# Message passing on sorted edges: one block of the last layer changes from gathered to multiplied

## The chip, the cores and the metric

The kernel runs on one core of a Trainium2 chip. The metric is the device time of one execution in microseconds; the time of a kernel is the median of its runs. The engines are PE (matrix multiplication; PEld is its weight load), DVE, ACT and POOL (elementwise work; POOL issues the indirect gathers here), and SP, which only issues DMAs here.

## The reference

A graph network on 6250 nodes of 256 features and 100000 edges that are sorted by destination. Four times the features of every edge's source are summed at its destination and added to the node's own, and a small network of three dense steps follows; the last of the four has a middle of 64 features.

```python
def agg(h):
    return jax.ops.segment_sum(h[src], dst, num_segments=N)
for l in range(NL - 1):
    h = x + agg(x)
    h = jax.nn.relu(h @ W1s[l] + b1s[l])
    h = jax.nn.relu(h @ W2s[l] + b2s[l])
    x = h @ W3s[l] + b3s[l]
h = x + agg(x)
h = jax.nn.relu(h @ cW1 + cb1)
h = jax.nn.relu(h @ cW2 + cb2)
return h @ cW3 + cb3
```

Ahead of it stands a layer norm with ReLU, and the input is added to the result.

## The kernel before

The nodes are cut into 49 blocks of 128. The sum over edges of a block of destinations is formed in one of two ways.

*Multiplied.* The counts of edges from every node to the block's 128 nodes are a matrix of small integers. It is built once, in layer 0, from one-hot matrices (`build`, L1053 one-hots on DVE, L1094 matmuls on PE, L1102 and L1104 to 8-bit integers on ACT and DVE), stored in HBM (`mats`), fetched again by SP in each layer (`fetch`), cast to the matmul's type (L1582, L1598, ACT and DVE in turn), and multiplied with all node features, which stay in SBUF as a high and a low part (`XY`). In layers 1 to 3 blocks 20 to 47 are multiplied as seven *panels* of four blocks (`product`, L1700, 196 matmuls each). A *solo* is a single block that is multiplied by itself (`product_by_node`, L1622, 49 matmuls); its result is kept until its quad of blocks is complete. In layer 0 blocks 18 to 43 are multiplied one by one on the same line (`teams`), while the build goes on; blocks 44 to 47 are only built there.

*Gathered.* For the other blocks, 17 indirect DMAs on POOL (`send`, L1407) bring the feature rows of 17 x 128 edges each from the layer's table in HBM, and one *visit* on PE (`add`, L1446, 23 small matmuls that the profile shows as 46) sums them with one-hot matrices. Block 48 is the last visit of every layer. Layer 0 has 23 visits, layers 1 and 2 have 20 each, layer 3 has 19 (blocks 0 to 17 and 48), 82 in all.

The sum of a group of four blocks is turned (L1506), and goes through the second dense step (`second`, L1248 in layer 3, L1256) and the third (`halves` L1268, `third` L1310, L1313); the first dense step needs no matmul of its own, since it is folded into the weights of the layer before. `given_out` adds the input (loaded by SP, L1287 and L1280 on DVE, result L1297) in layer 3.

All engines work in an order that the program fixes when it is built. PE's order comes from a planner with a clock of its own, in estimated microseconds: each matmul adds its cost (`passed`), a solo or panel is walked through matmul by matmul, and ahead of each group `meets` asks whether the next visit is due. `begin` plans the layer's gathers evenly, from now until the estimated end of the layer less `TAIL[l]`; `flow` puts a gather on POOL when its time has come, and makes it wait for the matmul that PE has just been given. From `ends[l] + LATE[l]` on, in steps of the walk, all visits left are due. `made` is the order in which blocks are built in layer 0, `order` the order of panels and solos in a layer, `place_of` tells where a built block lies in HBM. `spare` is the memory of `clT`, free after layer 0, in which solos' results and the last layer's weights are put. The lists `solos`, `made`, `order`, `TAIL` and `LATE` are those that the change touches.

Of the kernel before, what the change touches and what calls it, by code (L numbers as in the profile page):

```python
# [10 lines left out]
U8 = mybir.dt.uint8  # L11
# [6 lines left out]
P = 128  # L18
# [378 lines left out]
def sorted_edges(  # L397
# [39 lines left out]
    N, C = x.shape  # L437
    (E,) = src.shape
    NLAYER = W1s.shape[0]
# [27 lines left out]

    gone = [(0, 4), (4, 4), (8, 4), (12, 4), (16, 4), (44, 4), (48, 1)]
    panels = [(20, 4), (24, 4), (28, 4), (32, 4), (36, 4), (40, 4), (44, 4)]
    solos = [[], [19], [19], [18, 19]]  # L470
    stock = panels + [(b, 1) for b in max(solos, key=len)]
    place_of = {b + i: (p, i) for p, (b, n) in enumerate(stock) for i in range(n)}
    S0 = 2 * min(place_of)
# [2 lines left out]
    teams = [(18, 2), (20, 4), (24, 4), (28, 4), (32, 4), (36, 4), (40, 2), (42, 2)]  # L476
    made = [b + i for b, n in teams for i in range(n)]
    for i in range(panels[-1][1]):
        made.insert(6 * i + 5, panels[-1][0] + i)
    assert sorted(made) == sorted(place_of) and sum(gone[-3]) == panels[0][0] and gone[-2] == panels[-1] and all(n == gone[0][1] for _, n in gone[:-1]) and sorted(  # L480
        b + i for b, n in gone[:-2] + gone[-1:] + panels for i in range(n)) == list(range(NT))
    NQ = len(gone)
# [498 lines left out]
    with tc.manual_schedule():  # L981
        with tc.tile_pool(name="prep", bufs=2) as prep, tc.tile_pool(
            name="ps_t", bufs=2, space=PSUM
# [150 lines left out]
        def later(n, fn):  # L1134
            due.append((now[0] + n, fn))
# [378 lines left out]
        EARLY = 8  # L1514
        PRE = (GSUB + EARLY) // 2
        tails = [7] + [panels[-1][1] + gone[-1][1]] * (NLAYER - 1) + [panels[-1][1]]
        order = [[]] + [[0, 1, 2, 19, 3, 4, 5, 6]] * 2 + [[0, 1, 18, 2, 3, 19, 4, 5, 6]]
        order = [[p if p < len(panels) else place_of[p][0] for p in o] for o in order]
        nodes = [b + i for b, n in teams for i in range(n)]
        parts = [(j, 1) for j in range(NT)]  # L1520
# [11 lines left out]
        spare = clT.rearrange("p a q s -> p (a q s)").bitcast(F32)  # L1532
        sums = ps_g.tile([P, W], F32, name="sums")
        MARGIN = 6.0
        TAIL = [10.0] + [-5.0] * (NLAYER - 1) + [10.0]
        LATE = [-8] + [10] * (NLAYER - 1) + [-8]
        COLS, FULL32, TURN, VISIT, BUILD, BURST = 0.457e-3, 1.68e-3, 0.4, 3.0, 0.2, 0.3
        clock = [0.0]
        FAR, SPAN = 7, 6
# [137 lines left out]
        def product(l, p, ps_a):  # L1677
            b0, n = stock[p]
            if n == 1:
                k = solos[l][::-1].index(b0)  # L1680
                u = alone[l, b0] = late.tile([P, C], F32, name="us", bufs=1) if (
                    k == 1) else spare[:, k // 2 * C:(k // 2 + 1) * C]
                return product_by_node(l, (b0,), ps_a, [u], None)
            last = len(panels) - 1
            w = n * P
# [42 lines left out]
        with tc.tile_pool(name="hots", bufs=1) as hots, tc.tile_pool(  # L1728
            name="ats", bufs=1
        ) as ats, tc.tile_pool(name="rings", bufs=AHEAD + 2) as rings, tc.tile_pool(  # L1730
            name="gath", bufs=24
        ) as gath, tc.tile_pool(
            name="ps_a", bufs=2, space=PSUM
        ) as ps_a, tc.tile_pool(name="ps_b", bufs=3, space=PSUM) as ps_b:
            begun = {0: clock[0]}
            rings.tile([P, 64], U8, name="align", bufs=1)
            layers[0].begin()
            layers[0].send(8)
            beside = build(hots, ats, ps_b)
            while now[0] < PRE:  # L1740
                for _ in range(2):
                    next(beside)
                    built[0] += 1
                tick(layers[0])
                layers[0].advance()
            later(1, lambda: later(2, lambda bad=verdict(): judge(bad)))
            for team in teams:
                product_of_team(*team, ps_a, beside, team == teams[-1])
            assert next(beside, None) is None and built[0] == total
        chunks = ctx.enter_context(tc.tile_pool(name="chunks", bufs=1))  # L1750
        late = ctx.enter_context(tc.tile_pool(name="late", bufs=1))
        rings = ctx.enter_context(tc.tile_pool(name="rings2", bufs=AHEAD + 5))
        rings.tile([P, 128], U8, name="align", bufs=1)
        gath = ctx.enter_context(tc.tile_pool(name="gath2", bufs=27))
        ps_a = ctx.enter_context(tc.tile_pool(name="ps_a2", bufs=4, space=PSUM))
        for l in range(1, NLAYER + 1):
# [67 lines left out]
```

## Time and profile before

| | us |
|---|---|
| median of 3 runs (2122.25 to 2134.76) | 2123.33 |
| profiled execution, its own time | 2128.08 |
| its span, first to last instruction | 2126.3 |
| PE's busy time in the span | 2034.3 |
| POOL's busy time in the span | 1445.9 |
| first gather of layer 1 / 2 / 3 | 714.2 / 1194.9 / 1668.4 |

The page has one line for each group of instructions: line, engine, operation, out<-in with shapes, count, then busy time, mean ns of one, and the engine's idle time just before them with what ended it. In the chain of waits a line is start, length and what: the work, followed back from the last instruction, that each step waited for. A line of the timeline gives start, length, engine, line, operation, and in brackets the idle time before it and what ended that. Matmuls overlap, so the mean of one in the page is longer than the time from one to the next, which the chain shows.

### The profile page before, as it was taken

The numbers are of one execution on the slowest core, as the hardware profiler recorded it, in microseconds if no ns is written. First come the engines' busy times: TensorE is split into PE (matmuls) and PEld (weight loads), VectorE is DVE, ScalarE is ACT, GpSimd is POOL, SyncE is SP. The second block draws the span as 40 slices with busy tenths as digits, with TensorE's granted clock in tenths as the row PEclk, the third lists the DMA queues.
The fourth block names the chain that finished last, engine by engine and source line by source line (L and its number), as shares of the span: only waits on it lengthen the run. The fifth ranks groups of instructions, "written<-read, shape, count | busy, mean of one in ns | idle before, by whom it ended". The sixth has DMA issues, their size and how long they took to land.

```text
span 2126.3 us, 33236 instructions
## 1 busy us (share of the span) xinstructions
PE 2034.3 (96%) x12076; PEld 1495.9 (70%) x12076; DVE 925.0 (44%) x2103; ACT 872.8 (41%) x1793; POOL 1445.9 (68%) x1467
## 2 busy tenths in 40 slices
PE   6889999999999999999999999999999999989998
PEld 4657676667676777777777777777776767766665
DVE  6987767677662422232234322322233323223333
ACT  5766656456555433323233423232233322222222
POOL 3747777677774477777777477777776477777772
PEclk9989999999999999999999999999999999999999
DMA  5534455545455654555566554555555555555563
GB/s 174 159 117 148 145 156 150 157 139 162 140 161 168 205 163 145 160 177 161 154 184 202 171 165 149 176 166 158 169 171 176 173 170 185 161 184 185 154 189 109
DMA packets 184900, 347.54 MB, mean 163 GB/s; under 512 B 32446, under 2 KB 118496, under 8 KB 184726
## 3 DMA queue, kind: packets, MB, share of 16 engines
q0 software_dynamic: 68960, 185.36, 29.9%
q1 hardware_dynamic: 113838, 158.12, 22.8%
q8 instruction: 96, 1.57, 0.3%
q10 hardware_dynamic: 1928, 1.85, 0.3%
q14 instruction: 78, 0.64, 0.1%
HBM read 287.93 MB, written 57.26 MB: 162 GB/s over the span
## 4 chain that ended last, share of the span: by engine, by line
PE 86%; DMA 4%; DVE 3%; issue 1%; ACT 1%; POOL 1%; DVEq 0%; SPq 0%; POOLq 0%; ACTq 0%
PE agg L1700 43%; PE agg L1622 15%; PE sums L1446 11%; PE ps L1256 6%; PE ps L1313 6%; PE bp L1094 4%; DMA rows<-table,idx 4%; PE ps L1506 1%; DVE hi L1053 1%; POOL rows L1407 1%; DVE at L1104 1%; PE ps L1268 1%; PE ps L1248 0%; DVE lo L1053 0%; ACT at L1102 0%
## 5 line engine op out<-in xcount | busy, mean ns | idle before, releaser
L1407 POOL DMA_INDIRECT rows<-table,idx x1394 | 1388.8, 996 | 595.7 <-issue 225.7
L1700 PE MATMUL agg<-a,XY 128*128 128x512 f32 x4116 | 978.6, 395 | 1.9 <-DVE clT L1634 1.9
L1700 PEld LDWEIGHTS agg<-a,XY 128*128 128x128 f32 x4116 | 764.9, 188 | 192.7 <-issue 35.0
L1598 ACT CAST a<-at 128x512 fp32r<-128x512 uint8 (+1 forms) x542 | 328.7, 617 | 653.7 <-PE agg L1700 613.1
L1598 DVE CAST a<-at 128x512 fp32r<-128x512 uint8 x543 | 246.8, 456 | 515.7 <-PE agg L1700 479.1
L1622 PE MATMUL agg<-XY,a 128*128 128x512 f32 x1470 | 405.4, 410 | 1.7 <-ACT a L1582 1.0
L1622 PEld LDWEIGHTS agg<-XY,a 128*128 128x128 f32 x1470 | 260.0, 190 | 51.4 <-issue 6.6
L1446 PE MATMUL sums<-rows,hot 128*32 128x256 f32 x3772 | 248.3, 391 | 33.5 <-DMA rows<-table,idx 33.3
L1446 PEld LDWEIGHTS sums<-rows,hot 128*32 128x32 f32 x3772 | 124.0, 111 | 151.0 <-DMA rows<-table,idx 46.1
L1582 ACT CAST a<-at 128x512 fp32r<-128x512 uint8 (+2 forms) x362 | 197.2, 576 | 6.6 <-PE agg L1622 6.6
L1102 ACT CAST at<-bp 128x392 uint8<-128x392 f32 x252 | 121.5, 490 | 186.9 <-PE bp L1094 181.3
L1104 DVE CAST at<-bp 128x392 uint8<-128x392 f32 x228 | 128.6, 564 | 137.4 <-PE bp L1094 135.0
L1475 DVE TENSOR_TENSOR u<-u,sums 128x256 f32<-128x256 f32 x82 | 34.4, 419 | 301.3 <-PE agg L1700 273.6
L1094 PE MATMUL bp<-hi,lo 128*128 128x196 bf16 x960 | 128.3, 256 | 14.9 <-DVE hi L1053 13.3
L1313 PE MATMUL ps<-w,h 128*128 128x256 f32 x588 | 133.8, 379 | 1.4 <-ACT h L1259 0.9
L1053 DVE TENSOR_TENSOR hi<-cols,pairs 128x784 bf16<-128x784 bf16 x240 | 134.9, 562 | 0.0
L1256 PE MATMUL ps<-h,w 128*128 128x512 f32 (+3 forms) x332 | 133.8, 545 | 0.3 <-ACT h L1713 0.3
L1094 PEld LDWEIGHTS <-lo 128*128 128x128 bf16 x960 | 72.3, 100 | 83.5 <-DVE hi L1053 34.9
L1313 PEld LDWEIGHTS ps<-w,h 128*128 128x128 f32 x588 | 111.3, 190 | 18.5 <-ACT h L1259 1.4
L1321 DVE TENSOR_TENSOR zz<-ps,w 128x512 f32<-128x512 f32 (+1 forms) x75 | 50.2, 679 | 116.5 <-PE ps L1313 116.5
L1053 DVE TENSOR_TENSOR lo<-lanes,pairs 128x512 bf16<-128x512 bf16 x240 | 100.6, 419 | 0.7 <-issue 0.3
L1510 ACT ACTIVATE h<-ps,bias 128x256 f32<-128x256 f32 (+1 forms) x116 | 47.6, 464 | 128.5 <-PE ps L1506 128.5
(170 smaller groups left out, 962.6 us busy)
## 6 DMA issues: line engine op xcount, KB each, us to landing
at<-mat SPq DMA_DIRECT2D x151, 448.0 KB
mat<-at SPq DMA_DIRECT2D x30, 784.0 KB
rows<-table,idx POOLq DMA_INDIRECT x1394
table<-zz SPq DMA_DIRECT2D x72, 256.0 KB
back<-table SPq DMA_DIRECT2D x99, 128.0 KB
xs<-in_x_dram SPq DMA_DIRECT2D x8, 768.0 KB
table<-zs SPq DMA_DIRECT2D x24, 256.0 KB
out_dram<-zz SPq DMA_DIRECT2D x24, 256.0 KB
```

The source lines that it names most:

```text
L1053: nc.vector.tensor_tensor(o.rearrange("p q (n t) -> p q n t", t=2), values.rearrange("p (n t) -> p n t", t=2)[:, None, :, :].to_broadcast( ...
L1094: mm = nc.tensor.matmul(bp[:, m * HW:(m + 1) * HW], lo[:, q + m, :], hi[:, q + m, :], start=True, stop=True)
L1102: nc.scalar.copy(o, v)
L1104: nc.vector.tensor_copy(o, v)
L1256: mm = nc.tensor.matmul(ps[:mp, :w], weights[l][0][:, c, i * P:i * P + mp], h1[:, c, :w], start=(c == 0), stop=(c == KC - 1))
L1313: mm = nc.tensor.matmul(o, h2[0][:, c, nodes], w3[:, c, :], start=(c == 0), stop=(c == KC - 1))
L1407: got = nc.gpsimd.indirect_dma_start(out=t, out_offset=None, in_=tables[self.l][:, :], in_offset=bass.IndirectOffsetOnAxis(ap=idx[:, o:o + ...
L1446: nc.tensor.matmul(self.sums[m * Q:(m + 1) * Q, :C], self.hot[:, c - min(rounds), m, :], self.rows[g, c + 4 * m], start=(c == ROUNDS[0][0] ...
L1582: nc.scalar.copy(a[:, i * m * P:(i + 1) * m * P].rearrange("p (j d) -> p j d", j=m), counts[b][:, j:j + m, :])
L1598: cast(o, at[:, :, d:d + m * P])
L1622: mm = nc.tensor.matmul(agg, a[:, d:d + P], XY[:, j, :], start=(j == 0), stop=(j == NT - 1))
L1700: mm = nc.tensor.matmul(agg[c][:, :w], XY[:, j, o:o + P], a[:, :w], start=(at == 0 and half == 0), stop=(at == NT - 1 and half == 1))
```

## The change

Block 17 becomes a third solo of layer 3: it is built and stored in layer 0 (31 blocks built, 30 before), and in layer 3 it is multiplied (49 matmuls) and no longer gathered (18 visits, 17 gathers fewer). Layer 3's order of products has it between the first two panels. The blocks that are only built stand at other places of `made`. TAIL plans layer 0's visits 6 us sooner and layer 3's 13 us later, LATE makes layer 3's last visits due three steps later. Since `clT` begins two columns sooner, it grows by 128 bytes for each partition; the padding tiles keep what lies behind it where it was, and the solos' places in `spare` leave room for the weights.

```diff
-    solos = [[], [19], [19], [18, 19]]
+    solos = [[], [19], [19], [17, 18, 19]]
...
     for i in range(panels[-1][1]):
-        made.insert(6 * i + 5, panels[-1][0] + i)
+        made.insert((4, 9, 14, 19)[i], panels[-1][0] + i)
+    made.insert(25, 17)
...
-        order = [[]] + [[0, 1, 2, 19, 3, 4, 5, 6]] * 2 + [[0, 1, 18, 2, 3, 19, 4, 5, 6]]
+        order = [[]] + [[0, 1, 2, 19, 3, 4, 5, 6]] * 2 + [[0, 17, 1, 18, 2, 3, 19, 4, 5, 6]]
...
-        TAIL = [10.0] + [-5.0] * (NLAYER - 1) + [10.0]
-        LATE = [-8] + [10] * (NLAYER - 1) + [-8]
+        TAIL = [16.0] + [-5.0] * (NLAYER - 1) + [-3.0]
+        LATE = [-8] + [10] * (NLAYER - 1) + [-5]
...
-                    k == 1) else spare[:, k // 2 * C:(k // 2 + 1) * C]
+                    k == 1) else spare[:, 3 * (k // 2) * C:(3 * (k // 2) + 1) * C]
...
-            rings.tile([P, 64], U8, name="align", bufs=1)
+            rings.tile([P, 192], U8, name="align", bufs=1)
...
-        rings.tile([P, 128], U8, name="align", bufs=1)
```

From L479 on the lines of the changed kernel have numbers higher by one (L1446 becomes L1447, L1700 becomes L1701).

PE in the second half of layer 3, visits 13 to 15 of 19 in before (L1446 a visit, L1700 panel matmuls, L1506 turns, L1248 and L1268 dense steps):

```order
L1446 MATMUL sums<-rows,hot 32x256 x23
L1700 MATMUL agg<-a,XY 128x512 x52
L1268 MATMUL ps<-clT,h_19350 128x256 x4
L1700 MATMUL agg<-a,XY 128x512 x16
L1446 MATMUL sums<-rows,hot 32x256 x23
L1700 MATMUL agg<-a,XY 128x512 x44
L1506 MATMUL ps<-ident,u 128x128 x4
L1700 MATMUL agg<-a,XY 128x512 x4
L1248 MATMUL ps<-h_19590,w_16837 64x256 x4
L1700 MATMUL agg<-a,XY 128x512 x20
L1446 MATMUL sums<-rows,hot 32x256 x23
```

and in the changed kernel, visits 14 to 16 of 18:

```order
L1447 MATMUL sums<-rows,hot 32x256 x23
L1701 MATMUL agg<-a,XY 128x512 x44
L1507 MATMUL ps<-ident,u 128x128 x4
L1701 MATMUL agg<-a,XY 128x512 x4
L1269 MATMUL ps<-clT,h_19859 128x256 x4
L1701 MATMUL agg<-a,XY 128x512 x32
L1447 MATMUL sums<-rows,hot 32x256 x23
L1701 MATMUL agg<-a,XY 128x512 x80
L1249 MATMUL ps<-h_20198,w_16940 64x256 x4
L1447 MATMUL sums<-rows,hot 32x256 x23
```

Between two visits stood 68 panel matmuls; now there are 80.

PE at the end of the program, from the last visit on, in before (L1256 and L1310 are the dense steps of block 48; the last two rows are the last panel's):

```order
L1446 MATMUL sums<-rows,hot 32x256 x23
L1700 MATMUL agg<-a,XY 128x512 x8
L1506 MATMUL ps<-ident,u 128x128 x2
L1700 MATMUL agg<-a,XY 128x512 x4
L1248 MATMUL ps<-h_20413,w_16837 64x256 x4
L1700 MATMUL agg<-a,XY 128x512 x12
L1268 MATMUL ps<-clT,h_20534 128x256 x4
L1700 MATMUL agg<-a,XY 128x512 x12
L1256 MATMUL ps<-h_20522,w_16837 64x128 x2
L1700 MATMUL agg<-a,XY 128x512 x8
L1310 MATMUL ps<-clT,h_20595 128x256
L1700 MATMUL agg<-a,XY 128x512 x20
```

and now:

```order
L1447 MATMUL sums<-rows,hot 32x256 x23
L1701 MATMUL agg<-a,XY 128x512 x8
L1507 MATMUL ps<-ident,u 128x128 x2
L1701 MATMUL agg<-a,XY 128x512 x4
L1249 MATMUL ps<-h_20600,w_16940 64x256 x4
L1701 MATMUL agg<-a,XY 128x512 x12
L1269 MATMUL ps<-clT,h_20715 128x256 x4
L1257 MATMUL ps<-h_20705,w_16940 64x128 x2
L1311 MATMUL ps<-clT,h_20763 128x256
L1249 MATMUL ps<-h_20742,w_16940 64x256 x4
L1269 MATMUL ps<-clT,h_20779 128x256 x4
```

The last visit had 64 panel matmuls behind it and has 24; block 48's dense steps no longer stand among the panel's matmuls.

PE at the last two visits of layer 0 in before (L1622 products of single blocks, the last team):

```order
L1446 MATMUL sums<-rows,hot 32x256 x23
L1622 MATMUL agg<-XY,a 128x512 x24
L1506 MATMUL ps<-ident,un 128x128 x4
L1622 MATMUL agg<-XY,a 128x512 x12
L1506 MATMUL ps<-ident,u 128x128 x4
L1622 MATMUL agg<-XY,a 128x512 x12
L1256 MATMUL ps<-h_8171,w_1248 128x256 x4
L1446 MATMUL sums<-rows,hot 32x256 x23
L1622 MATMUL agg<-XY,a 128x512 x8
```

and now:

```order
L1447 MATMUL sums<-rows,hot 32x256 x23
L1623 MATMUL agg<-XY,a 128x512 x28
L1314 MATMUL ps<-w_1251,h_8080 128x256 x8
L1623 MATMUL agg<-XY,a 128x512 x8
L1507 MATMUL ps<-ident,un 128x128 x4
L1507 MATMUL ps<-ident,u 128x128 x4
L1623 MATMUL agg<-XY,a 128x512 x20
L1257 MATMUL ps<-h_8292,w_1249 128x256 x4
L1447 MATMUL sums<-rows,hot 32x256 x23
L1623 MATMUL agg<-XY,a 128x512 x8
```

The last but one visit stands sooner: between the two are 56 product matmuls and a third dense step, where there were 48.

## The prediction

> **What bounds the kernel now.** I read the page first, then the busy time by stage, the gather stream on POOL, and the chain of waits stage by stage.
>
> ```profile
> span 2126.3 us, 33236 instructions
> PE 2034.3 (96%) x12076; PEld 1495.9 (70%) x12076; DVE 925.0 (44%) x2103; ACT 872.8 (41%) x1793; POOL 1445.9 (68%) x1467
> 116.00:660.00 544.00, 526.84 (x3531) 371.60 (x3532) 380.29 (x864) 325.05 (x742) 385.14 (x383) 0.98 0.50 151
> 1170.00:1655.00 485.00, 480.05 (x2738) 357.81 (x2737) 146.26 (x313) 157.46 (x292) 337.19 (x340) 1.00 0.54 167
> 1655.00:2126.00 471.00, 437.39 (x2582) 322.46 (x2580) 147.04 (x306) 133.06 (x242) 319.88 (x323) 0.98 0.54 168
> ```
>
> After the span of a stage stand the busy times of PE, PEld, DVE, ACT and POOL, then granted clock, DMA share and GB/s. The 96% of PE is an average: in layer 0 (second row) PE works 527 of 544 us, in layer 2 480 of 485, in the last layer only 437 of 471. POOL's 320 us there look loose, but they aren't, because each gather is followed by a gap that is not counted as busy:
>
> ```profile
> 1194.88 1.28 POOL L1407 DMA_INDIRECT rows<-table,idx  x1 [26.13 <-PE agg L1700]
> 1635.60 0.96 POOL L1407 DMA_INDIRECT rows<-table,idx  x1 [0.30 <-issue]
> 1668.41 0.95 POOL L1407 DMA_INDIRECT rows<-table,idx  x1 [31.85 <-PE agg L1700]
> 2069.33 0.96 POOL L1407 DMA_INDIRECT rows<-table,idx  x1 [0.30 <-issue]
> 2091.71 0.97 POOL L1407 DMA_INDIRECT rows<-table,idx  x1 [0.31 <-issue]
> ```
>
> These are the first and last of layer 2's 340 gathers and the first, 306th and last of layer 3's 323. Layer 3: (2092.68 - 1668.41) / 323 = 1.3135 us a gather. Layer 2: (1636.56 - 1194.88) / 340 = 1.299. So 0.95 us of gather and 0.30 us of gap in nearly every turn: POOL runs without rest, and a visit (17 gathers) costs it 17 x 1.3135 = 22.3 us. The chain from the first visit of layer 3 to its 19th:
>
> ```profile
> by line: PE agg L1700 61.5%; PE sums L1446 13.1%; DMA rows<-table,idx 12.6%; PE agg L1622 4.9%; PE ps L1268 2.4%; PE ps L1248 2.0%; issue 1.5%; PE ps L1506 1.1%; POOL rows L1407 0.7%; ACT h L1510 0.1%
> ...
> 1692.35 2.73 PE sums L1446 x46
> ...
> 2069.33 6.76 DMA rows<-table,idx
> ...
> 2076.14 1.05 PE sums L1446 x10
> 2077.19 1.12 PE agg L1700 x4
> ...
> 2094.42 2.73 PE sums L1446 x46
> ```
>
> From visit 1 to 19 there are 402.1 us, 18 x 22.3: the visits stand exactly at POOL's pace, and the chain goes through landing gathers for 12.6% of it. How much of that PE loses follows from PE's own work, by these unit prices:
>
> ```profile
> 710.60 29.98 PE agg L1700 x132
> 1762.77 7.96 PE agg L1622 x35
> 1772.18 3.42 PE agg L1622 x14
> 1725.86 0.45 PE ps L1506 x4
> 1778.32 1.06 PE ps L1268 x8
> 1786.20 1.01 PE ps L1248 x8
> ```
>
> A panel matmul takes 29.98 / 132 = 0.227 us, a solo 7.96 + 3.42 = 11.4 us (0.232 each), a visit 2.73. Per four blocks the transposes, seconds and thirds take 0.45 + 1.01 + 1.06 = 2.5 us. In the built program stand between visits 1 and 19: 1136 panel matmuls (258.0 us), 98 of solos (22.8), 18 visits (49.1), ten groups of four (25.2), in all 355 us. So 402.1 - 355 = 47 us of layer 3 are waits, 2.6 for each visit. **The last layer is set by POOL's gathers, the layers before it by PE.**
>
> **The change, part by part.** *One block fewer gathered.* 17 gathers go, 306 are left. If the stream starts as before at 1668.41 and keeps 1.3135 us, its last gather ends at 1668.41 + 306 x 1.3135 = 2070.3 (the 306th of before did, 2069.33 + 0.96); at layer 2's 1.299 it ends at 2065.9. I take the first: same layer, same neighbours. From the last gather's end to the end of its visit (landing and the matmuls left) before shows 2077.19 - 2070.29 = 6.9 us above, and in layer 2
>
> ```profile
> 1640.00 1.51 PE sums L1446 x23
> 1641.51 2.04 PE agg L1700 x8
> ```
>
> 1641.51 - 1636.56 = 5.0. With the mean, 5.9, the last visit ends at 2076.2 (2071 to 2077). The Trainium skill, "DMA: Bandwidth & Descriptors", section "Anatomy of one DMA — SWDGE (gpsimd) path", has a fixed 2.0 us plus bytes / 436e3, an estimate of 2.3 us to landing for 128 KB; with the last third of a visit, about 1 us, the visit would end 2.6 us sooner than I say. The rows have the longer time, so I keep them.
>
> *PE's side of the same stretch.* Solo 17 adds 11.4 us, the visit that goes takes 2.7 away, and the rebuilt order moves 40 panel matmuls from behind the last visit ahead of it (64 stand behind it in before, 24 now; 12 of them go ahead of the first visit). First visit: 1692.35 + 12 x 0.227 = 1695.1. From there to the last: 1164 panel matmuls 264.3, 147 of solos 34.1, 17 visits 46.4, ten groups 25.2: 370 us. PE alone would end the last visit at 1695.1 + 370 + 2.7 = 2067.8, 8 us ahead of the gathers. A visit now has 21.8 us of PE work to 22.3 us of POOL's, in before 19.7: nearly level, POOL still the later.
>
> *Visits planned to the end.* Behind the last visit now stand 24 panel matmuls (5.5 us), two transposes (0.2) and four seconds (1.0): the panel ends at 2076.2 + 6.7 = 2082.9 instead of 2115.9. The plan pays for it behind that: block 48's and the quad's ends come behind the panel's instead of beside it. Rows for it:
>
> ```profile
> 2105.39 1.29 DVE L1297 TENSOR_TENSOR zz<-ps,xt 128x512 f32<-128x512 f32 x2 [2.45 <-PE ps L1268]
> 2099.57 1.29 DVE L1287 TENSOR_TENSOR xt<-xt,clT 128x512 f32<-128x512 f32 x2
> 2107.86 0.27 DVE L1284 MEMSET xt<- 128x256 f32 x1
> 2110.41 0.43 DVE L1287 TENSOR_TENSOR xt<-xt,clT 128x256 f32<-128x256 f32 x1 [2.27 <-DMA xt<-in_x_dram]
> 2111.61 0.42 DVE L1297 TENSOR_TENSOR zz<-ps,xt 128x256 f32<-128x256 f32 x1 [0.78 <-PE ps L1310]
> 2115.94 0.69 ACT L1713 ACTIVATE h<-agg,bias 128x512 f32<-128x512 f32 x1 [6.60 <-PE agg L1700]
> 2116.47 0.75 DVE L1710 TENSOR_SCALAR h<-agg,bias 128x512 f32<-128x512 f32 x1 [4.43 <-PE agg L1700]
> 2117.13 1.42 DVE L1280 TENSOR_TENSOR rows<-rows,clT 128x256 f32<-128x256 f32 x4
> 2119.72 1.42 DVE L1297 TENSOR_TENSOR zz<-ps,rows 128x256 f32<-128x256 f32 x4 [1.17 <-PE ps L1268]
> ```
>
> DVE's queue behind the panel is now: start 0.3, the panel's own bias 0.75, two L1287 (1.29), two L1297 (1.29), memset 0.27, then the load of block 48's input (2.27 from the memset to its use), 0.43 + 0.42, and the panel's 1.42 + 1.42: 9.9 us. PE's small matmuls run beside it, and on SP the panel's inputs are asked for within the last visit, some 10 us before their use. From the last addition (2121.1) to the end of the span (2126.3) before has 5.2 us. So 15.1 us stand behind the panel, 10.4 in before. The end: 2082.9 + 15.1 = 2098.0.
>
> *Layer 0: block 17 is built.* PE's 526.84 of 544 us leave no cover, so its chain price counts:
>
> ```profile
> L1094 PE MATMUL bp<-hi,lo 128*128 128x196 bf16 x960 | 128.3, 256 | 14.9 <-DVE hi L1053 13.3 <-ACT at L1102 1.2
> L1094 PEld LDWEIGHTS <-lo 128*128 128x128 bf16 x960 | 72.3, 100 | 83.5 <-DVE hi L1053 34.9 <-issue 27.3 <-DVE at L1104 15.1
> 651.49 2.80 PE L1446 MATMUL sums<-rows,hot 128*32 128x256 f32 x46
> 668.05 0.63 PE L1446 MATMUL sums<-rows,hot 128*32 128x256 f32 x6
> 671.07 4.46 PE L1446 MATMUL sums<-rows,hot 128*32 128x256 f32 x40 [2.38 <-DMA rows<-table,idx]
> ```
>
> 30 blocks are built in before, so one takes 128.3 / 30 = 4.3 us of matmuls, and at least 72.3 / 30 = 2.4 of weight loads; I take 4.3. Its DVE, ACT and store time lies beside PE (DVE 380 of 544). The longer TAIL[0] plans layer 0's visits 6 us sooner. The last one took 668.05 to 675.53, 7.5 us against 2.8 of an undisturbed one: 4.7 lost to a landing. In the built program its last gather was let go 3.4 us of PE work ahead of it, now 9.0; I take the whole 4.7 as gone (bounds 2 and 4.7). Layer 0 nets 4.3 - 4.7 = -0.4. Layers 1 and 2 have the same order of work: 0.
>
> *At nothing:* solo 17's casts and evacuation (DVE 147, ACT 133 of 471 us busy); its fetch, 784 KB, against 17 x 128 KB of gathers that go; the order of the builds; the padding tiles. Without that cover a cast would hold PE 0.5 us, some 7 us for the solo. A rule speaks against the casts: the Trainium skill, "SBUF — State Buffer", section "Who interferes with whom", lets DVE's copies in a two-port mode lock POOL out while it writes descriptors. The trace has gathers that fit:
>
> ```profile
> L1407 POOL DMA_INDIRECT rows<-table,idx x323: 947/953/1700, 1668.4 to 2091.7; - x162
> L1598 DVE CAST a<-at 128x512 fp32r<-128x512 uint8 x169 | 76.8, 456 | 160.8 <-PE agg L1700 146.7 <-PE agg L1622 13.3
> ```
>
> Shortest and median are 0.95 us, the longest 1.70. By that rule 7 more casts of 0.456 on DVE would cost POOL up to 3.2 us; the 13 us that layer 3's gathers lie above 0.95 in all (319.88 - 323 x 0.95) are in my 1.3135 already.
>
> *Sum:* 2098.0 - 0.4 = 2097.6, 28.7 us off the span. The profiled execution took 2128.08 us, 1.8 above its span, and lies 4.7 above the median of the three runs, 2123.33; taken off that: 2094.6.
>
> **The rivals.** A measurement of this kernel can tell about 1% (21 us) from no change.
>
> *Half of the waits stay (0.14).* Each gather is let go by a place on PE, some 7 to 9 us of PE's work ahead of its visit in the built program, before and now (4 us at the new last visit). If landing rather than POOL's pace holds the visits, a late visit holds the next gathers too. For it: landings of 5 to 7 us. Against: layer 2 has the same lead and PE loses 5 of 485 us. Price: 1.3 x 17 = 22 us on PE's 2067.8, instead of 8: 14 more, 2108.
>
> *All of the waits stay, slower than before (0.08).* The same with 2.6 us a visit: 2067.8 + 44 + 6.7 + 15.1 - 0.4 = 2133 of span, 7 more than before, 2130 us. It decides as soon as the 18 visits together lose more than 37 us. Against: in before POOL had no rest, which this needs to be chance.
>
> *Builds pace layer 0 (0.06).* If its length goes with the number of builds, one costs 544 / 30 = 18.1 us: 13.8 more, 2108. For: DVE hi ends 13.3 us of PE's idle time there. Against: PE idles 17 us there in all.
>
> The last visit might also end where it did (the plan without effect, 0.02): 2123.
>
> **How the numbers follow.** The forecast has 0.70: 2094, by its bounds 2084 (PE alone decides, builds at 2.4) to 2102 (casts on POOL, a landing of 6.9, 2 us of TAIL[0]'s gain). 0.67 of it is faster by over 1% (below 2102.1). Within 1%: the rest of it 0.03, half the waits 0.14, builds 0.06, no effect 0.02, and 0.04 of the slower case. Slower by over 1% (above 2144.5) needs all the waits and dear builds together: 0.04. The range 2084 to 2112 leaves out the slower case, the plan without effect and the edges, about 0.18; the likeliest case alone has 2084 to 2102.
>
> **What would show it.** In the profile after: 306 gathers of layer 3 at about 1.30 us, the last ending near 2070; waits of sums for rows in layer 3 under 15 us instead of 47; the panel ending 7 us behind the last visit and 15 from the end; layer 0's last visit near 2.8 us. Wrong would be: gaps on POOL in layer 3 well over 0.30 with waits on PE (the leads are too short), or layer 2's gathers starting over 5 us later than 1194.9 (layer 0).

## The result, and the profile after

The changed kernel takes 2110.11 us (median of four runs, 2109.16 to 2111.32), the kernel before beside it 2125.13 (four runs, 2122.25 to 2134.76): a ratio of 0.9922, with an interval of 0.990 to 0.9944. The gain is 15.0 us by the medians and 19.0 us by the spans of the two profiled executions. The 4 us between them are scatter: before's profiled execution lay 3.0 us above its median, after's 0.95 below its own. The forecast was 28.7 us, off the span and off the median alike.

The page of the changed kernel:

```profile
span 2107.3 us, 33354 instructions
PE 2038.2 (97%) x12111; PEld 1504.9 (71%) x12111; DVE 937.8 (45%) x2133; ACT 881.7 (42%) x1811; POOL 1435.5 (68%) x1450
```

and its busy time by stage (length, PE, PEld, DVE, ACT, POOL, clock, DMA share, GB/s):

```profile
116.00:666.00 550.00, 528.49 (x3557) 370.68 (x3556) 389.42 (x887) 330.52 (x756) 389.76 (x385) 0.98 0.50 150
1175.00:1661.00 486.00, 482.71 (x2744) 359.85 (x2744) 145.70 (x313) 158.85 (x294) 336.98 (x340) 1.00 0.54 167
1661.00:2107.00 446.00, 433.58 (x2583) 326.60 (x2581) 150.55 (x311) 137.44 (x249) 307.77 (x306) 0.99 0.56 174
```

In the last layer PE is busy for 434 of 446 us, where it was 437 of 471: the same work, with some 20 us less idling in it. What is left idle stands mostly behind the last visit. The groups of PE between the first and the last visit of layer 3 (busy us, mean ns | idle before, and what ended it) show where the idling went, first in before:

```profile
L1700 PE MATMUL agg<-a,XY 128*128 128x512 f32 x1137 | 268.8, 393 | 0.0
L1446 PE MATMUL sums<-rows,hot 128*32 128x256 f32 x832 | 64.2, 416 | 26.0 <-DMA rows<-table,idx 26.0
```

and in the changed kernel:

```profile
L1701 PE MATMUL agg<-a,XY 128*128 128x512 f32 x1165 | 274.5, 393 | 0.0
L1447 PE MATMUL sums<-rows,hot 128*32 128x256 f32 x785 | 49.9, 382 | 1.3 <-DMA rows<-table,idx 1.3
L1623 PE MATMUL agg<-XY,a 128*128 128x512 f32 x147 | 35.4, 394 | 0.0
```

An undisturbed visit takes 2.80 us from its first matmul to its last. Eighteen of them would be 50.4 us; before has 64.2 + 26.0, so 39.8 us went in visits that waited or were stretched. In the changed kernel it is 49.9 + 1.3 against 17 x 2.80 = 47.6: 3.6 us, and 2.3 more in the last visit, which lies outside the window. In the table below the same thing is counted from the visits' own lengths (39.4 and 5.5).

The end of the program on PE (start, us, idle before it and what ended that):

```profile
2079.86 0.63 PE L1447 MATMUL sums<-rows,hot 128*32 128x256 f32 x6
2081.33 1.93 PE L1447 MATMUL sums<-rows,hot 128*32 128x256 f32 x30 [0.84 <-DMA rows<-table,idx]
2083.95 1.05 PE L1447 MATMUL sums<-rows,hot 128*32 128x256 f32 x10 [0.69 <-DMA rows<-table,idx]
2084.93 2.12 PE L1701 MATMUL agg<-a,XY 128*128 128x512 f32 x8
2089.14 3.01 PE L1701 MATMUL agg<-a,XY 128*128 128x512 f32 x12
```

and on DVE:

```profile
2092.26 0.75 DVE L1711 TENSOR_SCALAR h<-agg,bias 128x512 f32<-128x512 f32 x1 [5.67 <-PE agg L1701]
2092.93 1.28 DVE L1288 TENSOR_TENSOR xt<-xt,clT 128x512 f32<-128x512 f32 x2
2094.13 1.28 DVE L1298 TENSOR_TENSOR zz<-ps,xt 128x512 f32<-128x512 f32 x2
2095.42 0.27 DVE L1285 MEMSET xt<- 128x256 f32 x1
2098.41 0.42 DVE L1288 TENSOR_TENSOR xt<-xt,clT 128x256 f32<-128x256 f32 x1 [2.73 <-DMA xt<-in_x_dram]
2098.93 0.43 DVE L1298 TENSOR_TENSOR zz<-ps,xt 128x256 f32<-128x256 f32 x1
2099.33 1.43 DVE L1281 TENSOR_TENSOR rows<-rows,clT 128x256 f32<-128x256 f32 x4
2100.68 1.41 DVE L1298 TENSOR_TENSOR zz<-ps,rows 128x256 f32<-128x256 f32 x4
```

The last visit runs from 2079.9 to 2085.0 and still waits twice for its rows (0.84 and 0.69 us). The panel ends 7.2 us behind it, at 2092.2, and DVE's queue then stands as the prediction listed it, with the load of block 48's input as the one wait (2.73).

Marks of all kernels, in us from the start of the span. "L0" is the time from the first product of layer 0 to the first panel matmul of layer 1, "waits L3" the visits' lengths above 2.80 us, summed over layer 3. "Panel ends" is the end of the last panel matmul. e1 to e4 are of one chip, e5 to e8 of a second and e9 to e12 of a third; which chip ran before and after is not known, but they keep the pace of e1 to e4 and are counted with the first:

| kernel | span | L0 | L0's last visit | first gather L3 | first visit L3 | last gather ends | last visit L3 | panel ends | waits L3 |
|---|---|---|---|---|---|---|---|---|---|
| before | 2126.3 | 556.2 | 7.48 | 1668.4 | 1692.3 | 2092.7 | 2094.4–2097.1 | 2116.4 | 39.4 |
| after | 2107.3 | 559.7 | 2.80 | 1674.1 | 1700.6 | 2080.7 | 2079.9–2085.0 | 2092.2 | 5.5 |
| e1_build_only | 2129.3 | 560.2 | 2.80 | 1674.0 | 1697.8 | 2095.8 | 2097.5–2100.3 | 2119.5 | 35.5 |
| e2_tail0 | 2124.7 | 554.2 | 2.80 | 1665.5 | 1689.4 | 2090.7 | 2092.4–2095.2 | 2114.4 | 40.1 |
| e3_old_plan | 2107.9 | 560.1 | 2.80 | 1675.1 | 1700.6 | 2074.4 | 2075.6–2078.4 | 2097.6 | 5.7 |
| e4_half_gathers | 2102.6 | 560.1 | 2.80 | 1674.6 | 1701.1 | 2074.3 | 2077.2–2080.0 | 2087.2 | −0.1 |
| e5_before_half | 2284.7 | 623.9 | 8.10 | 1866.2 | 1890.1 | 2246.5 | 2252.8–2255.6 | 2274.8 | −0.1 |
| e6_plan_alone | 2351.9 | 623.9 | 8.98 | 1854.8 | 1879.6 | 2326.1 | 2323.8–2329.7 | 2338.1 | 67.5 |
| e7_old_tail0 | 2348.9 | 630.6 | 7.88 | 1867.3 | 1893.8 | 2322.4 | 2321.7–2326.7 | 2333.9 | 48.9 |
| e8_after_again | 2351.0 | 622.9 | 2.80 | 1863.0 | 1889.5 | 2324.3 | 2323.8–2327.6 | 2334.8 | 51.2 |
| e9_after_third | 2351.4 | 629.1 | 2.80 | 1869.4 | 1895.9 | 2325.3 | 2324.1–2328.7 | 2335.8 | 47.7 |
| e10_old_plan | 2349.7 | 626.2 | 2.80 | 1859.0 | 1884.6 | 2312.1 | 2317.3–2320.1 | 2339.3 | 49.2 |
| e11_old_tail0 | 2352.8 | 630.5 | 8.03 | 1865.5 | 1892.0 | 2326.0 | 2324.7–2328.9 | 2336.0 | 47.2 |
| e12_solo_alone | 2348.1 | 625.2 | 7.84 | 1861.7 | 1887.3 | 2313.1 | 2316.1–2318.9 | 2338.1 | 55.2 |

From before to after, mark by mark: the first gather of layer 3 starts 5.7 us later, the last visit ends 12.1 us sooner, the panel 24.2 us sooner, and the end of the span is 15.1 us behind the panel instead of 9.9. That makes the 19.0. (The prediction's 2115.9 for before's panel is the start of ACT's first operation on its result; the last matmul ends 0.4 later.)

So two things had to be explained: why the gain is only half of the forecast by the medians and two thirds by the spans, and whether the waits that are left in layer 3 are the forecast's (gathers at POOL's pace, just behind PE), the rival's (late landings hold half of them), or neither.

### The profile page after: what moved, and what is told of

It is laid out like the page before. It is cut to its first block, busy times and chain, and to the rows that moved or that the text cites. A ratio compares the mean times of both kernels' runs of the same rounds, so it can differ in the third digit from the quotient of the medians.

```text
span 2107.3 us, 33354 instructions
## 1 busy us (share of the span) xinstructions
PE 2038.2 (97%) x12111; PEld 1504.9 (71%) x12111; DVE 937.8 (45%) x2133; ACT 881.7 (42%) x1811; POOL 1435.5 (68%) x1450
## 3 DMA queue, kind: packets, MB, share of 16 engines
q10 hardware_dynamic: 1928, 1.85, 0.3%
## 5 line engine op out<-in xcount | busy, mean ns | idle before, releaser
L1701 PE MATMUL agg<-a,XY 128*128 128x512 f32 x4116 | 976.6, 394 | 1.9 <-DVE clT L1635 1.9
L1701 PEld LDWEIGHTS agg<-a,XY 128*128 128x128 f32 x4116 | 765.2, 188 | 190.1 <-issue 32.4
L1599 DVE CAST a<-at 128x512 fp32r<-128x512 uint8 (+1 forms) x550 | 250.3, 457 | 522.2 <-PE agg L1701 476.0
L1623 PE MATMUL agg<-XY,a 128*128 128x512 f32 x1519 | 420.9, 410 | 1.7 <-ACT a L1583 1.0
L1623 PEld LDWEIGHTS agg<-XY,a 128*128 128x128 f32 x1519 | 268.3, 189 | 54.1 <-issue 9.2
L1447 PE MATMUL sums<-rows,hot 128*32 128x256 f32 x3726 | 234.6, 384 | 6.3 <-DMA rows<-table,idx 6.3
L1447 PEld LDWEIGHTS sums<-rows,hot 128*32 128x32 f32 x3726 | 119.1, 110 | 115.3 <-issue 29.7
L1314 PE MATMUL ps<-w,h 128*128 128x256 f32 x588 | 135.2, 382 | 1.4 <-ACT h L1260 0.9
L1314 PEld LDWEIGHTS ps<-w,h 128*128 128x128 f32 x588 | 112.4, 192 | 18.7 <-ACT h L1260 1.3
```

Source lines behind the costliest of these rows:

```text
L1314: mm = nc.tensor.matmul(o, h2[0][:, c, nodes], w3[:, c, :], start=(c == 0), stop=(c == KC - 1))
L1447: nc.tensor.matmul(self.sums[m * Q:(m + 1) * Q, :C], self.hot[:, c - min(rounds), m, :], self.rows[g, c + 4 * m], start=(c == ROUNDS[0][0] ...
L1599: cast(o, at[:, :, d:d + m * P])
L1623: mm = nc.tensor.matmul(agg, a[:, d:d + P], XY[:, j, :], start=(j == 0), stop=(j == NT - 1))
L1701: mm = nc.tensor.matmul(agg[c][:, :w], XY[:, j, o:o + P], a[:, :w], start=(at == 0 and half == 0), stop=(at == NT - 1 and half == 1))
```

## The experiments

**First chip: one part of the change at a time.** In this group the kernel before has a median of 2130.39 us (19 runs).

*The built block and layer 0's plan, without the rest.* Block 17 is built but stays gathered in layer 3, whose plan is the old one.

```diff
-    solos = [[], [19], [19], [17, 18, 19]]
-    stock = panels + [(b, 1) for b in max(solos, key=len)]
+    solos = [[], [19], [19], [18, 19]]
+    stock = panels + [(b, 1) for b in (17, 18, 19)]
...
-        order = [[]] + [[0, 1, 2, 19, 3, 4, 5, 6]] * 2 + [[0, 17, 1, 18, 2, 3, 19, 4, 5, 6]]
+        order = [[]] + [[0, 1, 2, 19, 3, 4, 5, 6]] * 2 + [[0, 1, 18, 2, 3, 19, 4, 5, 6]]
...
-        TAIL = [16.0] + [-5.0] * (NLAYER - 1) + [-3.0]
-        LATE = [-8] + [10] * (NLAYER - 1) + [-5]
+        TAIL = [16.0] + [-5.0] * (NLAYER - 1) + [10.0]
+        LATE = [-8] + [10] * (NLAYER - 1) + [-8]
```

> Block 17 is built and stored in layer 0, with the new order of builds and TAIL[0] 16, but layer 3 stays as before: 19 gathered blocks, two solos, old TAIL and LATE. Theory A (layer 0 pays for the build: about 9 us for the block, 4.7 back from the last visit): layer 1's first gather near 720.6 as in the changed kernel, layer 3 as long as before, span 6 us over before, 2132. Rival B (the 6 us by which layer 1 began later in the changed kernel come from that execution and not from the build): first gather near 714, span near 2126.

Measured: 1.0013 [1.0002, 1.0025], 2132.53 us; span 2129.3, 3.0 above before's (the first theory had 6; layer 3's visits wait 3.9 us less here). Layer 0 takes 560.2 us instead of 556.2.

*Layer 0's plan alone*, in the kernel before:

```diff
-        TAIL = [10.0] + [-5.0] * (NLAYER - 1) + [10.0]
+        TAIL = [16.0] + [-5.0] * (NLAYER - 1) + [10.0]
```

> Before with TAIL[0] 16 alone: layer 0's visits are planned 6 us sooner, no block more is built. Theory A (the last visit's wait of 4.7 us goes and nothing else changes): last visit of layer 0 2.8 us long, layer 1's first gather at 709.5, 4.7 us off the span. Rival B (sooner visits cost layer 0 what they gain, since gathers and one-hots stand closer): first gather at 713 to 716, no change of the span.

Measured: 0.9991 [0.9982, 1.0001], 2127.88 us; layer 0 takes 554.2 us. The ends of layer 0 and the start of layer 1 on PE, in before:

```profile
690.81 1.21 PE L1700 MATMUL agg<-a,XY 128*128 128x512 f32 x4 [1.85 <-DVE clT L1634]
691.86 3.62 PE L1313 MATMUL ps<-w,h 128*128 128x256 f32 x16
```

in e2:

```profile
672.29 2.80 PE L1446 MATMUL sums<-rows,hot 128*32 128x256 f32 x46
690.35 1.19 PE L1700 MATMUL agg<-a,XY 128*128 128x512 f32 x4 [1.85 <-DVE clT L1634]
691.38 3.62 PE L1313 MATMUL ps<-w,h 128*128 128x256 f32 x16
```

and in the changed kernel:

```profile
676.96 2.80 PE L1447 MATMUL sums<-rows,hot 128*32 128x256 f32 x46
694.97 1.46 PE L1701 MATMUL agg<-a,XY 128*128 128x512 f32 x4 [1.85 <-DVE clT L1635]
696.22 5.07 PE L1314 MATMUL ps<-w,h 128*128 128x256 f32 x16
```

with the busy time of its engines behind that point (length, PE, PEld, DVE, ACT, POOL, clock, DMA share, GB/s):

```profile
696.00:701.50 5.50, 5.50 (x20) 4.53 (x19) 0.86 (x2) 0.00 (x0) 0.00 (x0) 0.71 0.07 25
```

What follows: the last visit of layer 0 takes 2.80 us as soon as TAIL[0] is 16, as forecast, so its whole wait of 4.7 goes. But layer 0 gets only 556.2 − 554.2 = 2.0 us shorter by it; the other 2.7 are given back on the way. (Layer 1's first gather in e2, at 713.8, is where the rival expected it; layer 0 itself began 1.5 us later in that execution.) The built block, with the order that it makes, costs 560.2 − 554.2 = 6.0 us where 4.3 were put down. The price of layer 0 is thus +3.5 to +4.0 us for the two together, not −0.4. The timed medians agree in sign (+2.1 us for e1, −2.5 for e2), though e2's interval includes no change at all.

Where the 6.0 us lie is in the group of the build's matmuls in layer 0, first in e2, then in e1:

```profile
L1094 PE MATMUL bp<-hi,lo 128*128 128x196 bf16 x912 | 118.3, 250 | 9.4 <-DVE hi L1053 8.6 <-ACT at L1102 0.2
L1095 PE MATMUL bp<-hi,lo 128*128 128x196 bf16 x944 | 123.0, 251 | 12.4 <-DVE hi L1054 11.6 <-DVE at L1105 0.2 <-ACT at L1103 0.2
```

The 32 matmuls of the new block are 4.7 us busy there, near the 4.3 that were forecast, and in part overlap with other work; but PE also idles 3.0 us more ahead of the group, all of it until DVE has made one-hots. That is the part of the build that the prediction let lie beside PE. The start of layer 1 is slower, too: its 16 matmuls of L1314 take 5.07 us instead of 3.62, at a granted clock of 0.71 in that stretch. Every kernel with the built block shows it on this chip (5.07 to 5.30), before and e2 do not.

*Layer 3 planned as before*, all else as in the changed kernel:

```diff
-        TAIL = [16.0] + [-5.0] * (NLAYER - 1) + [-3.0]
-        LATE = [-8] + [10] * (NLAYER - 1) + [-5]
+        TAIL = [16.0] + [-5.0] * (NLAYER - 1) + [10.0]
+        LATE = [-8] + [10] * (NLAYER - 1) + [-8]
```

> The changed kernel with layer 3's old TAIL (10) and LATE (-8): three solos, 18 visits, but planned to 13 us ahead of the end. Theory A (POOL's pace decides the last visit at about 2081 all the same, the panel work that then stands behind it comes after it, and PE waits ahead of the visits): the waits of sums for rows in layer 3 grow from 4 to 12 us or more, span 5 us longer than the changed kernel, 2112. Rival B (PE decides layer 3, so the places of the visits are free): waits under 6 us, span 2107, or 5 less, since the tail behind the panel is 10.4 us again instead of 15.

Measured: 0.9895 [0.9878, 0.9911], 2108.97 us; span 2107.9 against 2107.3, waits of layer 3 5.7 us against 5.5. Its group of visits:

```profile
L1447 PE MATMUL sums<-rows,hot 128*32 128x256 f32 x783 | 51.3, 388 | 2.4 <-DMA rows<-table,idx 2.4
```

What follows: the first theory's 12 us of waits or more are not there, and the rival's marks (under 6 us, 2107) are; with the block gone, the old plan has no more waits than the new one. The last visit stands sooner and ends at 2078.4 without a wait, 6.6 us before the changed kernel's, but 19.2 us of panel work stand behind it instead of 7.2. What the plan wins at the panel's end (5.4 us) goes again behind the panel (15.1 instead of 10.3). **The plan of the last layer shows no gain on this chip**, as far as two executions and medians from different groups (the changed kernel was not timed beside e3) can tell; what the change gains here is there without it.

*Half the gathers of layer 3 left out*, in the changed kernel: every second gather of that layer is not sent, and the visits' matmuls read the rows of the gather before it. All of PE's work is left as it is.

```diff
+                    if self.l == NLAYER and k % 2:
+                        self.rows[g, k] = self.rows[g, k - 1]
+                        self.sent += 1
+                        continue
```

> The changed kernel without every second gather of layer 3: the odd ones of a block's 17 are left out and the visit reads the rows of the one before again, so PE's work and order are the same and POOL has 162 gathers there instead of 306. Theory A (after the change PE's own work decides layer 3): only the 4 us of waits and lengthened visits go, span 2102 to 2104. Rival B (half of before's waits, some 20 us, are still in layer 3): span near 2087. Both: no idle time of sums for rows is left in layer 3.

Measured: 0.9881 [0.9865, 0.9898], 2105.63 us; span 2102.6, 4.7 us below the changed kernel's. Its groups between first and last visit:

```profile
L1705 PE MATMUL agg<-a,XY 128*128 128x512 f32 x1165 | 274.5, 393 | 0.0
L1451 PE MATMUL sums<-rows,hot 128*32 128x256 f32 x782 | 47.6, 381 | 0.0
```

What follows: with 162 gathers instead of 306 no visit waits (47.6 us are 17 x 2.80), and the layer still takes 2077.2 − 1701.1 = 376.1 us from the first visit to the last. This is PE's own time, and it decides this layer: all the waiting for gathers that is left in the changed kernel is worth 4.7 us of its span. This excludes the rival "half of the waits stay", though its 2108 us is nearer to the measured 2110 than the forecast: it had 22 us of waits left, and there are 5.5. That holds for this chip.

**Second chip: the same question put to the kernel before, and the plans again.** Before takes 2371.62 us here (25 runs), 11% more than on the first chip. Visits are long in every layer there: those of the changed kernel (e8) take 10.8, 37.0, 62.7 and 51.2 us more than 2.80 each, in layers 0 to 3. The spans expected below are the first chip's and do not hold here.

*Half the gathers left out of layer 3 in the kernel before* (the same four lines):

> Before without every second gather of layer 3 (the odd ones of a block's 17 are left out and the visit reads the rows of the one before again): PE's work and order are before's, POOL has 171 gathers there instead of 323. Theory A (39 us of before's layer 3 are waits for gathers, and they are what the change took away): span near 2087, visits of layer 3 2.8 us long, and the difference to the changed kernel with half its gathers (2102.6) is the price of the change on PE, 15 to 17 us. Rival B (the half clock that the profile shows in layer 3 of before costs by itself and stays): span 2095 or more.

Measured: 0.9628 [0.959, 0.9666], 2278.19 us. Its groups between the first and the last visit of layer 3:

```profile
L1704 PE MATMUL agg<-a,XY 128*128 128x512 f32 x1137 | 268.9, 393 | 0.0
L1450 PE MATMUL sums<-rows,hot 128*32 128x256 f32 x829 | 50.8, 381 | 0.0
```

What follows: PE's prices are the same on both chips (268.9 us for 1137 panel matmuls here, 268.8 on the first), so the waitless stretch may be carried over. From first to last visit PE needs 2252.8 − 1890.1 = 362.7 us of its own in before. The first chip's 402.1 us therefore held 39.4 us of waits, not the 47 of the prediction, which had put PE's own work at 355. The same visits' lengths gave 39.4 by themselves. The rival's lower clock does not stay either: in this stretch the granted clock is 1.00.

*The new plan of layer 3 in the kernel before*, with block 17 still gathered:

```diff
-        TAIL = [10.0] + [-5.0] * (NLAYER - 1) + [10.0]
-        LATE = [-8] + [10] * (NLAYER - 1) + [-8]
+        TAIL = [10.0] + [-5.0] * (NLAYER - 1) + [-3.0]
+        LATE = [-8] + [10] * (NLAYER - 1) + [-5]
```

> Before with the new TAIL (-3) and LATE (-5) of layer 3 alone, two solos and 19 gathered blocks. Theory A (where POOL decides the last visit, panel work that is moved ahead of it fills waits; the plan is worth something there and nothing where PE decides): last gather still ends near 2093 to 2096, the panel ends 7 us behind the last visit, span 2118 to 2121. Rival B (gathers are let go by PE's places, so visits planned later let them go later and the stream ends as much later): last gather near 2102, span 2126 or more.

Measured: 0.9964 [0.9937, 0.9992], 2360.17 us. *The changed kernel with layer 0's old plan* (TAIL's first entry back to 10), *and the changed kernel itself* as its measure on this chip:

> The changed kernel with layer 0's old TAIL (10). Theory A (sooner visits in layer 0 take the last visit's wait away but cost nearly the same on the way, as with TAIL[0] alone): last visit of layer 0 again 5 us or more long, but layer 1's first gather within 2 us of the changed kernel's 720.6, span 2106 to 2110. Rival B (TAIL[0] is worth the 4.7 us that the prediction gave it): first gather near 725, span 2112.

> The changed kernel itself, to have it beside the others on one chip. Both theories: span 2106 to 2109, visits of layer 3 4 to 7 us longer in all than 2.8 each, 0.7 to 0.9% under before.

Measured: 0.9931 [0.9905, 0.9957], 2350.51 us, and 0.9916 [0.9887, 0.9945], 2352.48 us.

What follows: where layer 3's visits are long (67.5 us above 2.80 each in e6), planning them to the end is worth something by itself, 0.4% with an interval that stays just below 1. Which of the two theories on the stream of gathers holds is open, since the kernel before has no trace on this chip. TAIL[0]'s part shows in layer 0's last visit (7.88 against 2.80 us) but not in the time: e7's and e8's intervals cover one another. Layer 0 itself is 7.7 us longer in e7's traced execution than in e8's, but two executions with the same layer 0 on the third chip, e11 and e12, differ by 5.3.

**Third chip: the change taken apart once more.** Before: 2366.4 us (15 runs). The changed kernel again, with layer 3's old plan (the edit of e3), with layer 0's old plan (that of e7), and with both:

> The changed kernel once more, as the measure for the three runs beside it. Where gathers land as in the first executions (1.3 us from one to the next): 0.7 to 0.9% under before, visits of layer 3 with 4 to 7 us of waits in all. Where they land as slowly as in the run e8_after_again (1.5 us): some 50 us of waits, and again about 0.8%.

> The changed kernel with layer 3's old TAIL and LATE, beside the changed kernel. Theory A (where PE decides layer 3 the plan is worth nothing): within 0.15% of it if gathers land in 1.3 us; 6 to 10 us slower than it if they land in 1.5 us, since panel work then stands behind a late last visit. Rival B (the old plan is better in itself, as the run e3_old_plan let one think): 3 us or more faster.

> The changed kernel with layer 0's old TAIL, beside the changed kernel. Theory A (TAIL[0] is worth little where gathers land quickly): layer 1's first panel matmul within 2 us of the changed kernel's and the time within 0.1%. Rival B (it is worth the 4.7 us of the prediction): first panel matmul 4 to 6 us later, 0.2% slower.

> Block 17 as a solo with both old TAILs and the old LATE: the change without its planning. Theory A (the block itself brings all of the gain): within 0.2% of the changed kernel, 0.6 to 1.0% under before. Rival B (the plans carry the gain): 10 us or more above the changed kernel.

Measured: e9 0.9908 [0.9883, 0.9933], 2348.28 us; e10 0.9938 [0.9914, 0.9962], 2352.69; e11 0.9921 [0.9893, 0.9949], 2352.18; e12 0.995 [0.9931, 0.997], 2354.19.

What follows: of 18.1 us that the whole change gains here (2366.4 − 2348.28), the block that is no longer gathered brings 12.2 by itself, and the two plans together some 6, by medians whose intervals just touch. Each plan taken back alone is worth about 4 us by the medians, with intervals that overlap, so their shares stay open; so does the second chip's tie of e7 and e8. None of the three runs hit the marks of its first theory: e10's 4.4 us are short of the 6 to 10, e11's 3.9 us (0.17%) are nearer to its rival's 0.2%, and e12's 5.9 us are just outside 0.2%. Layer 3's visits are long on this chip, too. The group of visits of e9 ("issue" is idle time for which the profile shows no wait):

```profile
L1447 PE MATMUL sums<-rows,hot 128*32 128x256 f32 x783 | 79.0, 384 | 14.9 <-issue 11.3
```

By 79.0 + 14.9 − 47.6 the visits are 46 us longer than undisturbed ones, with the very program that has 3.6 on the first chip. The gathers of layer 3 on POOL, in the changed kernel on the first chip:

```profile
L1408 POOL DMA_INDIRECT rows<-table,idx x306 | 307.8, 1006 | 130.0 <-issue 52.4 <-PE agg L1701 37.8 <-DMA w<-in_L_gnn_cW_dram 31.2
```

and in e9:

```profile
L1408 POOL DMA_INDIRECT rows<-table,idx x306 | 304.2, 994 | 185.1 <-issue 65.7 <-PE agg L1701 63.7 <-DMA w<-in_L_gnn_cW_dram 33.4
```

with one of its gathers in the timeline:

```profile
2004.56 0.95 POOL L1408 DMA_INDIRECT rows<-table,idx  x1 [2.82 <-PE agg L1701]
```

POOL works no longer for them (304 us against 308); it idles 55 us more, 26 of them until PE's panel matmuls let the next gather go; the last row shows one such wait of 2.82 us. So PE holds POOL here. That would be the ring of the rival "half of the waits stay" if the gathers landed late in their turn and held PE, but the trace's DMA records speak against it. From a gather's start to its last packet pass 2.6 us in the median in e9, and 2.7 in the changed kernel on the first chip. In 13 of e9's 18 visits of layer 3 all 17 gathers had landed before the visit's first matmul, and these 13 hold 35.5 of the 47.7 us. On the first chip no such visit is long: the 11 of the changed kernel and the 6 of before take 2.80 us each. One of the 13, whose last packet ended at 2096.8:

```profile
2098.40 2.39 PE L1447 MATMUL sums<-rows,hot 128*32 128x256 f32 x32
2101.09 1.10 PE L1447 MATMUL sums<-rows,hot 128*32 128x256 f32 x5 [0.29 <-issue]
2102.53 0.62 PE L1447 MATMUL sums<-rows,hot 128*32 128x256 f32 x4 [0.34 <-issue]
2103.95 1.10 PE L1447 MATMUL sums<-rows,hot 128*32 128x256 f32 x5 [0.80 <-issue]
```

Its second half goes in steps of 0.7 to 1.4 us with no wait that the profile names. The gathers have a part in it, since e5's visits of layer 3, with half of them left out, take 2.80 us on such a chip; but what stretches the visits there is not shown.

## Why the prediction was right in its direction and too large in its size

Against the forecast's span of 2097.6 the changed kernel's 2107.3 is 9.7 us long: 5.9 before the first visit of layer 3 (1700.6, forecast 1695.1 − 0.4 = 1694.7; 0.6 of it was there when layer 0 began), 3.3 between there and the end of the last visit (384.4 us, forecast 2075.8 − 1694.7 = 381.1), 0.5 behind it (22.3 us, forecast 21.8). By the medians another 4 us of gain are missing, the scatter of the two profiled executions told above. The measured 2110 lies outside the likeliest case's own 2084 to 2102, and the gain of 0.8% is not the one of over 1% that had 0.67. It lies within 2084 to 2112 only because that range was kept open for two rivals at 2108, and the runs exclude both as mechanisms on this chip: that the time lies in the range is in part luck.

- **Layer 0, "4.3 − 4.7 = −0.4": the term that failed most.** It measured +3.5 in the changed kernel. The step that was wrong is "I take the whole 4.7 as gone": the wait went, but a wait at the last visit isn't the layer's loss when the visits ahead of it move too; 2.0 us of it reached layer 1. That was the lower bound given, and e2 shows it. The block's 4.3 us (matmuls alone) measured 6.0 with its new order of builds. The step that fails here is "Its DVE, ACT and store time lies beside PE": in e1 PE idles 3.0 us more than in e2 ahead of the build's matmuls, until DVE's one-hots are made. Whether the block or the new order of builds makes these waits was not separated; no run has the one without the other. The rival "builds pace layer 0" at 18.1 us each is excluded by the same pair. With 6.0 and 2.0 the sum would have been 4.4 us later. The mark that the prediction set for this step tripped: layer 2's gathers start at 1201.1, 6.2 us later than in before.
- **Layers 1 and 2, "0".** Layer 1's first gathers come 25.6 us behind its first panel matmul instead of 23.4. Of these 2.2 us, 1.7 are the panel matmuls and the L1314 group of the rows above, at the lower clock. The two layers together then gain back 0.7 us.
- **"355 us, so 47 us of waits": the wrong size in layer 3.** 355 came from 0.227 us a panel matmul, taken from one undisturbed stretch of 132. Over the whole stretch e4 and e5 give 0.232 and 0.234, when all that is not a panel matmul is taken off at the prediction's prices ((376.1 − 105.7) / 1164 and (362.7 − 97.1) / 1136). The trace of before has it directly: from the start of each panel matmul to the start of what follows it, the 1136 take 265.0 us, not 258.0. The change's own difference came out about right: 13.4 us where 15 were forecast.
- **"PE alone would end the last visit 8 us ahead of the gathers"** fell with that size. From the measured first visit, PE alone ends it at 1700.6 + 376.1 + 2.8 = 2079.5; the gathers at POOL's forecast pace would end it at 1674.1 + 306 x 1.3135 + 5.9 = 2082.0. The two are level within 2.5 us, and measured it ended at 2085.0, because the plan lets the last gathers go late: they came 1.329 us apart, (2080.68 − 1674.13) / 306, while e3, which plans them sooner, had them 1.305 apart and its last visit without a wait.
- **The panel and the end** were right: 7.2 us from the last visit to the panel's end (forecast 6.7), 15.1 from there to the end of the span (forecast 15.1). e3 shows the price of it: the old plan has 10.3 there.
- **"At nothing".** The evacuation, the casts and the fetch of solo 17 leave no wait in layer 3's groups. The gathers' mean did go from 0.990 us (319.88 / 323) to 1.006: 4.8 us over 306, where the prediction had estimated up to 3.2 from the casts' own times. That the casts are the cause is not shown: e3, with the same casts, has 0.996, and e2, without them, 0.995. The rule that it drew on (the Trainium skill, "SBUF — State Buffer", section "Who interferes with whom") lets DVE's casts in a two-port mode lock POOL out; the trace points to another operation of DVE. Of the changed kernel's 1377 gathers 40 took over 1.4 us; all 40 overlap a DVE operation with two inputs, and 36 of them the visits' one-hots (L1431), which only 110 gathers overlap at all. e4 bounds what all this can cost here by its 4.7 us.

What was right: that the last layer was held by its gathers, that taking 17 of them away and giving PE 11 us of products in their place frees PE of nearly all its waits, and that this reaches the end of the program. What stays open: whether the new order of builds or the block itself makes PE wait for one-hots, what stretches the visits on the second and third chip, what TAIL[0] is worth there, and how the plans share their 6 us on the third. No version was shown to beat the changed kernel: e3's interval overlaps that of the change on the first chip, and on the third chip the same edit (e10) has the slower median.

## What to carry to other kernels

Where two engines run nearly level, price the waits from a run that takes one of them away (half the transfers, the other engine's work untouched), not as a stage's length less a sum of best-case unit prices: 2 to 3% on the unit price of a thousand matmuls was 7 of the 8 us of waits that didn't exist. A wait that disappears in one place is worth only what reaches the next stage's start, so read that mark. And a predicted number that is hit says nothing of its mechanism: the rival that landed nearest was one whose mechanism the runs excluded on that chip. Nor is a long visit yet a late transfer: whether its rows had landed is in the DMA records.

## What the runs showed of the hardware

- **The same program takes 11% longer on two other chips.** The changed kernel takes 2348 to 2352 us there instead of 2110, and its gathers in layer 3 start 1.49 to 1.51 us apart instead of 1.33. Undisturbed panel matmuls (268.9 and 268.8 us for 1137) and landings (2.5 and 2.6 us in the median, 2.7 on the first chip) keep their times. Of the 244 us between the two spans (e8 against the changed kernel's first execution) some 147 are longer visits; why they are longer is open. The gain was 0.8 to 0.9% on all three chips.
- **A matmul is dearer where the work changes.** Between starts of single matmuls in the trace of the changed kernel, a panel matmul behind another one takes 0.228 us, behind a visit 0.34 (55 cases), behind a dense step 0.40 (71 cases; 0.33 in layer 3), and ahead of a visit 0.32, each a mean. This is what the 0.227 left out.
- **Short stretches at a lower clock.** The granted clock was 0.71 in the 5.5 us behind layer 1's first panel matmuls, and 0.58 in 4 us behind the wait of layer 0's last visit in before, whose 40 matmuls left take 4.46 us there (a whole visit of 46 takes 2.80):

```profile
672.00:676.00 4.00, 4.00 (x30) 1.91 (x24) 0.00 (x0) 0.00 (x0) 0.00 (x0) 0.58 0.00 0
1976.00:1990.00 14.00, 9.04 (x63) 4.94 (x61) 2.75 (x6) 1.24 (x2) 9.61 (x10) 0.76 0.68 208
```

The second row is a stretch of before's layer 3 in which PE worked 9 of 14 us. The Trainium skill, "TensorE: Matmul & The Clock Gate", section "What's actually happening", halves PE's clock after an idle window of some 3.4 us; the rows agree that waits and lower clock go together in layer 3. They do not say why the 1.85 us wait at layer 1's start brings it in the kernels with the built block on the first chip and not in before and e2, which wait as long there. The built block is not its condition: on the second chip the 16 matmuls behind that wait take 4.98 and 5.13 us in e5 and e6, which do not build it.
